# A row-product loop on one core: four larger pieces, two buffers, an even engine split, and semaphores reset in four stages

**Chip, cores, metric.** One core of one Trainium2 chip. The metric is device time in microseconds (us) of one execution; medians of several fast runs unless said otherwise. Runs of one kernel agree here within 0.05%, so differences of one or two us can be read.

## The reference

```python
# inputs: r_inputs, float32, (4096, 256)
dot = jnp.einsum('bi,bj->bij', inputs, inputs)
iu, ju = jnp.triu_indices(256)
return dot[:, iu, ju]            # float32, (4096, 32896)
```

Each row of 256 numbers becomes its 32,896 products x_i * x_j with i <= j. The output is 539 MB, the input 4 MB. So this is a kernel that writes.

## The kernel before

A round takes 256 rows (two per partition). Its 32,896 columns are cut into pieces; for each piece VectorE and ScalarE fill a buffer and SyncE stores it. Round 0 stands ahead of the loop, the other fifteen are its iterations.

```python
REPEAT = 2; PIECES = 6; BUFS = 3; BUDGET = 0.95
...
def split(block, budget):   # the first rows of a piece go to ScalarE until
    ...                     # VectorE's time for the rest is within the budget (ns per output element)
...
borders = even_borders(0, width, PIECES)
x_out = [v.rearrange("(p g r) c -> g p r c", p=P, r=REPEAT)
         for v in dram_disjoint_views(out, PIECES)]
...
def round_of_rows(g, first):
    for c, (lo, hi) in enumerate(zip(borders, borders[1:])):
        o = opool.tile([P, REPEAT, hi - lo], F32, tag=f"o{c % BUFS}", name=f"o{c}")
        ...   # ScalarE: one ACTIVATE per matrix row i and per r;  VectorE: one product for one or two rows i
        dest = x_out[c][bass.ds(g, 1), :, :, a:b].rearrange("o p r c -> p (o r) c")
        nc.sync.dma_start(dest, o[:, :, a - lo : b - lo])
...
with tc.For_i(1, groups, 1, ..., iteration_sync="reg_based") as g:
    copies(xt[:, bass.ds(g, 1)]...)      # x of this round to xv (VectorE) and xa (ScalarE)
    round_of_rows(g, first=False)
```

Of the kernel before, what the change touches and what calls it, by code (L numbers as in the profile page):

```python
# [1 line left out]

# [5 lines left out]

F32 = mybir.dt.float32
AF = mybir.ActivationFunctionType  # L10
ALU = mybir.AluOpType

P = 128
UNIT = 64
REPEAT = 2
PIECES = 6
BUFS = 3
BUDGET = 0.95
FIRST = [512, 1536, 3584]


def even_borders(lo: int, hi: int, pieces: int) -> list[int]:
    units = (hi - lo) // UNIT
    return [lo + units * c // pieces * UNIT for c in range(pieces)] + [hi]


def runs(d: int, lo: int, hi: int) -> list:


    found, at = [], 0  # L30
    for i in range(d):
        a, b = max(at, lo), min(at + d - i, hi)
        if a < b:
            found.append((i, i + a - at, a, b - a))
        at += d - i
    return found


def vector_ops(block: list) -> list:




    ops, k = [], 0
    while k < len(block):
        i, j, at, n = block[k]
        m = 2 if k + 2 < len(block) and i == j else 1
        ops.append((block[k], m))
        k += m
    return ops  # L50


def interleave(block: list) -> list:


    half = len(block)
    while half and len(vector_ops(block[:half])) > len(vector_ops(block[half:])):
        half -= 1
    a, b = vector_ops(block[:half]), vector_ops(block[half:])
    return [op for k in range(max(len(a), len(b))) for ops in (a, b) for op in ops[k : k + 1]]  # L60


def vector_time(block: list) -> float:
    return sum(68 + 1.046 * REPEAT * n * m for (*_, n), m in vector_ops(block))


def split(block: list, budget: float) -> int:


    scalar, k = 0.0, 0  # L70
    while k < len(block):
        scalar += REPEAT * (184 + 0.837 * block[k][3])
        if vector_time(block[k:]) <= budget or scalar > vector_time(block[k + 1 :]):
            break
        k += 1
    return k


def window(ap: bass.AP, free: list) -> bass.AP:
    return bass.AP(ap.tensor, ap.offset, [list(ap.ap[0]), *free])  # L80


@with_exitstack
def kernel(
    ctx: ExitStack, tc: tile.TileContext, x: bass.AP, out: bass.AP
):







    nc = tc.nc
    n, d = x.shape
    width = out.shape[1]
    assert n % (P * REPEAT) == 0 and width == d * (d + 1) // 2 and width % UNIT == 0
    groups = n // (P * REPEAT)
    borders = even_borders(0, width, PIECES)

    xpool = ctx.enter_context(tc.tile_pool(name="x", bufs=1))
    opool = ctx.enter_context(tc.tile_pool(name="o", bufs=1))


    x_out = [
        v.rearrange("(p g r) c -> g p r c", p=P, r=REPEAT)
        for v in dram_disjoint_views(out, PIECES)
    ]


    each, total = REPEAT * d, n // P * d
    xt = xpool.tile([P, groups, each], F32, name="x")
    x_in = x.rearrange("(p g r) d -> p g (r d)", p=P, r=REPEAT)
    xv = xpool.tile([P, each + 1], F32, name="xv")
    xa = xpool.tile([P, each], F32, name="xa")
    nc.vector.memset(xv[:, each:], 0.0)  # L116
    cuts = [0, 1, groups // 2, groups]
    for a, b in zip(cuts, cuts[1:]):
        nc.sync.dma_start(xt[:, a:b], x_in[:, a:b])

    def copies(x_now):
        nc.vector.tensor_copy(xv[:, :each], x_now)  # L122
        nc.scalar.activation(xa, x_now, AF.Copy)  # L123

    def round_of_rows(g, first: bool):
        for c, (lo, hi) in enumerate(zip(borders, borders[1:])):
            o = opool.tile([P, REPEAT, hi - lo], F32, tag=f"o{c % BUFS}", name=f"o{c}")
            start = first and c == 0
            cuts = [lo, *(FIRST if start else []), hi]
            for a, b in zip(cuts, cuts[1:]):  # L130
                block = runs(d, a, b)
                k = split(block, 0.0 if start else BUDGET * REPEAT * (b - a))
                for i, j, at, length in block[:k]:
                    for r in range(REPEAT):
                        nc.scalar.activation(  # L135
                            o[:, r, at - lo : at - lo + length],
                            xa[:, r * d + j : r * d + j + length],
                            AF.Copy,
                            scale=xa[:, r * d + i : r * d + i + 1],
                        )  # L140
                for (i, j, at, length), m in interleave(block[k:]):
                    at -= lo
                    nc.vector.tensor_tensor(  # L143
                        o[:, :, at : at + m * length],
                        window(xv[:, j:], [[d, REPEAT], [1, m], [1, length]]),
                        window(xv[:, i:], [[d, REPEAT], [1, m], [0, length]]),
                        ALU.mult,
                    )
                dest = x_out[c][bass.ds(g, 1), :, :, a:b].rearrange("o p r c -> p (o r) c")
                nc.sync.dma_start(dest, o[:, :, a - lo : b - lo])  # L150

    copies(xt[:, 0])
    round_of_rows(0, first=True)

    with tc.For_i(  # L155
        1,
        groups,
        1,
        hint_engines=[],
        head_align_engines=[mybir.EngineType.DVE, mybir.EngineType.Activation],  # L160
        iteration_sync="reg_based",
    ) as g:
        copies(xt[:, bass.ds(g, 1)].rearrange("p o d -> p (o d)"))
        round_of_rows(g, first=False)


# [1 line left out]
_INS = ["r_inputs"]  # L168
_OUTS = [((4096, 32896), "float32")]


# [20 lines left out]
```

## Time and profile before

| | before |
|---|---|
| median time | 1279.12 us |
| span of the profiled run | 1277.3 us |
| VectorE / ScalarE busy | 79% / 40% |
| DMA engines busy (share of 16 engines' span) | 99.7% |

The span is what the profile shows of one execution; timed runs stand about 2 us above it. The store is the bound: the 16 DMA engines never rest, and the compute engines wait for buffers. The prediction below shows the lines for this. The DMA queue's own waits say what SyncE, which issues every store, waits for (in total, how many times, longest):

```profile
SPq L150 <- DVE o L143: 1183.4, 99, 14.0
SPq L155 <- DMA out_dram<-o: 27.4, 3, 13.0
```

SyncE (SPq) waits for the computing of a piece and for next to nothing else: 4.5 us in all for ScalarE's copies of x, and the very end of the program (L155 is the loop's line). Waiting there is harmless: two stores are already under way or queued.

### The profile page before, as it was taken

The page shows a single profiled execution, that of the slowest core. Times are in us where ns is not written, and L with a number is a line of the kernel's source. Part 1 is how long each engine was busy: PE and PEld are TensorE (multiplying, and loading weights), DVE is VectorE, ACT ScalarE, POOL GpSimd, SP SyncE. Part 2 cuts the span into 40 slices and gives each one's busy share as a digit, 9 for nine tenths or more (in the row PEclk, how much of TensorE's full clock was granted, in tenths as well). Part 3 has the DMA queues.
Part 4 walks back from the last instruction along what each step waited for, and adds up shares of the span by engine and source line. Part 5 has one row for each costly group of instructions (what it writes and reads, how often), then busy time and mean ns, then how long its engine had stood idle before and what let it go on. Part 6 is the DMA issues. An engine that isn't in the chain of part 4 may idle for free.

```text
span 1277.3 us, 6155 instructions
## 1 busy us (share of the span) xinstructions
DVE 1006.2 (79%) x1877; ACT 504.7 (40%) x1591; POOL 0.2 (0%) x4
## 2 busy tenths in 40 slices
DVE  8978787887878788787878878787887878788780
ACT  5433435335252352623526244352433524344340
POOL 0000000000000000000000000000000000000000
DMA  9999999999999999999999999999999999999997
GB/s 385 433 432 430 433 432 429 429 429 428 428 428 429 429 429 428 427 428 429 429 428 428 429 428 429 428 428 428 429 429 429 428 428 429 429 429 427 428 428 327
DMA packets 27365, 543.21 MB, mean 425 GB/s; under 512 B 1632, under 2 KB 1632, under 8 KB 2528
## 3 DMA queue, kind: packets, MB, share of 16 engines
q1 hardware_dynamic: 27360, 543.17, 99.7%
q14 instruction: 5, 0.04, 0.0%
HBM read 4.19 MB, written 538.97 MB: 425 GB/s over the span
## 4 chain that ended last, share of the span: by engine, by line
DMA 67%; ACT 12%; issue 10%; DVE 9%; ACTq 0%; DVEq 0%; SPq 0%
DMA out_dram<-o 67%; ACT o L135 11%; DVE o L143 9%; ACT xa L123 0%; DMA x<-in_r_inputs_dram 0%; ACTq L123 0%; DVEq L143 0%; SPq L150 0%; ACTq L155 0%; ACTq L135 0%; DVE xv L122 0%
## 5 line engine op out<-in xcount | busy, mean ns | idle before, releaser
L143 DVE TENSOR_TENSOR o<-xv 128x760 f32<-128x760 f32 (+56 forms) x1860 | 999.4, 616 | 228.9 <-DMA out_dram<-o 223.1
L135 ACT ACTIVATE o<-xa 128x253 f32<-128x253 f32 (+48 forms) x1574 | 493.3, 403 | 738.5 <-DMA out_dram<-o 707.9
L122 DVE COPY xv<-x 128x512 f32 (+1 forms) x16 | 6.8, 427 | 11.5 <-DVE o L143 7.7
L123 ACT ACTIVATE xa<-x 128x512 f32 (+1 forms) x16 | 10.1, 630 | 3.2 <-DMA x<-in_r_inputs_dram 1.6
L123 ACT ACT_TABLE_LOAD x1 | 1.3, 1283 | 0.7 <-PEq L179 0.7
L116 DVE MEMSET xv<- 128x1 f32 x1 | 0.1, 59 | 0.8 <-PEq L179 0.8
L179 POOL MEMSET const-uint8-127<- 128x1 uint8 x1 | 0.1, 103 | 0.0
L179 POOL MEMSET const-bfloat16-1.0<- 128x1 bf16 x1 | 0.1, 102 | 0.0
L179 POOL MEMSET const-float32-0.0<- 128x1 f32 x1 | 0.1, 99 | 0.2 <-issue 0.2
L179 POOL MEMSET const-float32-1.0<- 128x1 f32 x1 | 0.1, 99 | 0.0
## 6 DMA issues: line engine op xcount, KB each, us to landing
out_dram<-o SPq DMA_DIRECT2D x64, 5504.0 KB, 28.5
out_dram<-o SPq DMA_DIRECT2D x31, 5440.0 KB, 28.9
x<-in_r_inputs_dram SPq DMA_DIRECT2D x1, 2048.0 KB, 12.2
out_dram<-o SPq DMA_DIRECT2D x1, 2048.0 KB, 12.2
out_dram<-o SPq DMA_DIRECT2D x1, 1856.0 KB, 13.8
x<-in_r_inputs_dram SPq DMA_DIRECT2D x1, 1792.0 KB, 6.7
out_dram<-o SPq DMA_DIRECT2D x1, 1024.0 KB, 10.3
out_dram<-o SPq DMA_DIRECT2D x1, 512.0 KB, 9.8
```

What stands on the lines that cost most here:

```text
L116: nc.vector.memset(xv[:, each:], 0.0)
L122: nc.vector.tensor_copy(xv[:, :each], x_now)
L123: nc.scalar.activation(xa, x_now, AF.Copy)
L135: nc.scalar.activation(o[:, r, at - lo : at - lo + length], xa[:, r * d + j : r * d + j + length], AF.Copy, scale=xa[:, r * d + i : r * d ...
L143: nc.vector.tensor_tensor(o[:, :, at : at + m * length], window(xv[:, j:], [[d, REPEAT], [1, m], [1, length]]), window(xv[:, i:], [[d, REP ...
L179: nc = _bacc.Bacc("TRN2", target_bir_lowering=False, num_devices=1)
```

## The change

The intent: fewer, larger packets for the DMA engines; room for the larger buffers by having two of them in place of three; ScalarE takes more of the work, so that a piece is ready in time with two buffers; and the loop's semaphores (the counters by which engines and DMA queues tell each other that something is done) are set back in four stages, one per piece, in place of register arithmetic on every wait.

```diff
-PIECES = 6
-BUFS = 3
-BUDGET = 0.95
+PIECES = 4
+LAST = 7552
+BUFS = 2
+BUDGET = 0.7
...
-    borders = even_borders(0, width, PIECES)
+    borders = [*even_borders(0, width - LAST, PIECES - 1), width]
...
         for c, (lo, hi) in enumerate(zip(borders, borders[1:])):
+            if c and not first:
+                tc.stage_boundary()
...
-        iteration_sync="reg_based",
+        iteration_sync="staggered",
```

## The prediction

> **What bounds the kernel now.** I read the page first (busy shares, slices, queues), then the waits, then one iteration on the timeline, then the windows at the end, then the trace's own packet and landing records. From the page:
>
> ```profile
> DVE 1006.2 (79%) x1877; ACT 504.7 (40%) x1591; POOL 0.2 (0%) x4
> DMA  9999999999999999999999999999999999999997
> ...
> DMA packets 27365, 543.21 MB, mean 425 GB/s; under 512 B 1632, under 2 KB 1632, under 8 KB 2528
> ...
> q1 hardware_dynamic: 27360, 543.17, 99.7%
> q14 instruction: 5, 0.04, 0.0%
> ```
>
> Neither compute engine is full; the 16 DMA engines are busy 99.7% of the span. The waits say the same from the other side:
>
> ```profile
> ACT o L135 <- DMA out_dram<-o: 707.9, 90, 10.1
> DVE o L143 <- DMA out_dram<-o: 223.1, 88, 3.6
> ```
>
> VectorE and ScalarE wait for buffers that the store has not yet released. One iteration on the timeline (piece 0 and piece 5 of 6):
>
> ```profile
> 1091.97 3.29 ACT L135 ACTIVATE o<-xa 128x256 f32<-128x256 f32 x8 [1.97 <-DMA out_dram<-o]
> 1091.99 10.07 DVE L143 TENSOR_TENSOR o<-xv 128x1008 f32<-128x1008 f32 x11 [1.41 <-DMA out_dram<-o]
> ...
> 1157.57 10.96 DVE L143 TENSOR_TENSOR o<-xv 128x340 f32<-128x340 f32 x44 [2.99 <-DMA out_dram<-o]
> 1157.58 10.61 ACT L135 ACTIVATE o<-xa 128x44 f32<-128x44 f32 x40 [7.65 <-DMA out_dram<-o]
> ```
>
> A piece takes VectorE 10 to 11 us; its store takes 16 packets per DMA engine of 0.822 us = 13.15 us. So a gap of about 3 us follows every piece, and the store never runs dry. The end shows one thing more:
>
> ```profile
> 1265.00:1270.00 5.00, 0.00 (x0) 0.00 (x0) 0.00 (x0) 1.00 0.86 370
> 1270.00:1272.00 2.00, 0.00 (x0) 0.00 (x0) 0.00 (x0) 1.00 0.08 33
> 1272.00:1274.00 2.00, 0.00 (x0) 0.00 (x0) 0.00 (x0) 1.00 0.05 22
> 1274.00:1276.00 2.00, 0.00 (x0) 0.00 (x0) 0.00 (x0) 1.00 0.03 11
> ```
>
> The last columns are DMA share and GB/s. 0.06 is one engine of 16: one DMA engine works on alone to 1275.24, while the other fifteen end between 1269.4 and 1270.4 (packet records). **One laggard** sets the end. The sixteen landings of each store show it falling behind by some 0.33 us once per iteration; its packets take 0.84 to 0.85 us instead of 0.813, seen in the iteration I opened while piece 5, the one with many small instructions (84 in 11 us), is computed, and return to 0.82 us when that ends.
>
> **What the Trainium skill says.** "DMA: Bandwidth & Descriptors", section Bandwidth (Where 436 GB/s comes from): 16 ports give 435.2 GB/s. The trace agrees: steady slices hold 427 to 433. Same page, Why small descriptors are slow: each packet carries a fixed overhead. The trace agrees and gives the size: median packets of 2048, 4096 and 8192 B take 84, 159 and 309 ns, so 75 ns per 2048 B (27.3 B/ns) and 9 ns fixed; at 21,760 and 22,016 B the medians are 813 and 822, which is 27.2 B/ns plus 13 ns. Same page, Specifications: about 0.6 us to the first byte on this path. The trace has 1.03 us from the start of the first load's issue (0.74) to its first packet (1.77); I use 1.03. From a last packet to its landing it has 0.44 us (1275.24 to 1275.67). "Runtime: NRT & Kernel Launch", Instruction fetch mechanics: an engine holds 512 instructions and fetches when a branch leaves them. The trace agrees as far as it goes: VectorE runs 235 instructions per iteration, the five instruction packets inside the span all fall before 130 us, and no back edge stalls. The changed loop is shorter on VectorE (about 100) and about 150 on ScalarE, so I expect no fetch stall. I found no page that prices resets in stages.
>
> **The change, part by part.**
>
> (1) Larger pieces. Borders become three of 8448 columns and one of 7552. A packet is one row of a piece: 33,792 or 30,208 B instead of 22,016 or 21,760. Per DMA engine, there were 256 rows x 6 = 1536 output packets; there will be 1024. 512 fewer at 9 to 13 ns is 4.6 to 6.7 us, all of it on the path, because the store is the path. Worked the long way per DMA engine: loads 9.8 us as now; first piece 16 x (0.084 + 0.159 + 0.309 + 0.728) = 20.5; 47 stores x 16 x 1.2555 = 944.1; 16 stores x 16 x 1.1236 = 287.6; start 1.8. Sum 1263.8 us. The same sum for the kernel before is 1269.9, which is where its fifteen engines end. So **minus 6.1 us**.
>
> (2) Two buffers and the even split. Computing piece c+1 may start only when store c-1 has landed, and store c+1 must be queued before store c ends. Prices: a VectorE product takes 68 ns + 1.046 ns per element (piece 0 before: 8844 elements in 11 instructions give 10.0 us, measured 10.07); a ScalarE row takes 184 ns + 0.837 ns per element (8 of 254 give 3.2, measured 3.29). Applied to the new split, VectorE / ScalarE: piece 0: 11.7 / 10.2; piece 1: 11.7 / 11.5; piece 2: 12.5 / 12.2; piece 3: 13.9 / 13.2 us. Before, piece 5 ran both engines side by side for 10.6 us at these prices, so I charge no contention. Piece 0 adds the copies of x (0.43 on VectorE, 0.63 on ScalarE), so 12.1. Around the computing: landing 0.44, first packet 1.03 after the issue, and some 0.5 to 1 us for the stage boundary (my estimate; semaphore steps on SyncE cost 0.05 to 0.1 us each in the tail, and before, computing began 0.1 us after a landing). Cover: store 3 lasts 16 x 1.124 = 18.0 us, the others 20.1. Worst cases: piece 3: 13.9 + 2.2 = 16.1 against 20.1; piece 0: 12.1 + 2.2 = 14.3, with the back edge (0.54 now) 14.9, against 18.0. **Slack 3 to 4 us, so 0 us added.** At the start the loads hold the queue until 13.6 us and the three small chunks until 22.2; the large fourth chunk (4864 columns) is computed by about 17, so nothing is lost there.
>
> (3) Resets in stages. What is removed is 104 register instructions per iteration on VectorE and the old bookkeeping at the back edge, neither of which the store waits for. What is added is, at each of four boundaries, a wait of every engine that the stage two back is finished, with SyncE waiting for the store of two pieces ago. With two buffers that is the very landing the computing waits for anyway. **About 0 us**, some tenths out of the slack of (2).
>
> (4) The laggard: 5.3 us now. If its delay follows bursts of small instructions, the last stage (98 in 14 us, no register instructions) is a gentler burst than 84 plus its register work in 11 us. I take 3.5 us, between 1 and 6: **minus 1.8**.
>
> Sum: 1263.8 + 3.5 + 0.44 landing + 1.6 closing = 1269.3 us of span. Timed runs stand 1.8 us over the profiled span (1279.12 against 1277.3), so 1271.1; I say **1271 us**, 0.6% less.
>
> **The rivals.** (a) A new wait: the boundary costs far more than I think, or computing in pieces 3 and 0 is slower with both engines full. Above 3 to 4 us of excess per stage the store runs dry: every further us in one stage costs 15 us, so 2 us in each of two stages make 1330. For it: two buffers leave only one store queued, and ScalarE goes from 40% to some 60% busy. Against it: the measured piece 5 with both engines full, and 3 us of slack. (b) The packet term fails: large packets run at the same bytes per ns as now, since the overhead might grow with size (9 ns at 8 KB, 13 at 22 KB); then only the laggard moves, and the time is 1275 to 1279. (c) The laggard grows: its cause is not settled by this trace, and a new layout might hit it more often; twice its lag is 1278 or so. With one store queued the fast engines would then idle for it, but the laggard itself would not, so nothing more is added. (d) Faster by 2%, under 1253.5, would need the ceiling itself: 543.17 MB at 435.2 GB/s is 1248 us, plus 1.8 start and 3.8 for landing, closing and timing gives 1253.7. Hardly possible.
>
> **Range and chances.** Without any laggard I get 1267.6; with (b) and the lag of now, 1279. The range is 1266 to 1278. Slower by 2% (above 1304.7) needs (a) at over 25 us in all: 0.05. Faster by 2%: 0.01. The rest, 0.94, is within 2%.
>
> **What would show it.** Right: DMA share 9 in every slice again and 429 to 431 GB/s; median packet of 33,792 B at 1.25 to 1.26 us; VectorE about 800 us and ScalarE about 760 us busy; every computing stage followed by an idle of 4 to 8 us whose releaser is the store (or a stage semaphore that follows it); issue to landing near 26 us; fifteen DMA engines ending near 1264 and one some us later. Wrong: slices with the DMA share at 8 or less (a), packets of 1.262 us or more (b), a single-engine tail longer than 6 us (c), or a boundary that delays the first product by more than 3 us after a landing.

## The result

The changed kernel takes **1295.74 us** (1295.56 to 1295.83), the kernel before 1279.12: 1.3% slower, where 0.6% faster was predicted, and outside the range. The ratio of the fast runs is 1.013 (interval 1.0112 to 1.0147). Ratios here are the mean time of one kernel's fast runs over that of the other's of the same rounds, so not quite the ratio of the medians.

The page of the changed kernel:

```profile
DVE 813.3 (63%) x1607; ACT 772.7 (60%) x2319; POOL 0.2 (0%) x4
...
DMA  9999999999999999999999999999999999999999
GB/s 386 436 432 434 433 394 435 406 419 433 407 435 406 435 428 396 435 406 435 428 398 433 406 435 427 414 418 406 435 425 416 430 395 434 423 418 429 411 419 406
...
q1 hardware_dynamic: 18656, 543.17, 97.9%
q14 instruction: 5, 0.04, 0.0%
```

Busy times came out as predicted (about 800 and 760 us were forecast). The ten-step digits of the DMA row are all 9, as before, and mislead: 9 means 90% or more. The row of rates shows it: every few slices it falls to 394 to 419 GB/s, and the queue is at 97.9% instead of 99.7%. In the kernel before, the slices between the start and the end held 427 to 433:

```profile
GB/s 385 433 432 430 433 432 429 429 429 428 428 428 429 429 429 428 427 428 429 429 428 428 429 428 429 428 428 428 429 429 429 428 428 429 429 429 427 428 428 327
```

What SyncE waits for has changed:

```profile
SPq L153 <- DVE o L146: 664.0, 53, 21.2
SPq L158 <- DMA out_dram<-o: 309.1, 45, 8.6
SPq L153 <- DMA out_dram<-o: 244.1, 14, 17.5
```

L153 is the line that issues a store. Fourteen times, once per iteration after the first, SyncE waits there not for computing but for **another store** to land, 17.5 us at the longest (counted from SyncE's arrival at the line, so most of it is harmless). L158 is the loop's line, the stage boundaries; those 45 waits were foreseen. One such place on the timeline, first all engines, then SyncE alone (start, duration, engine, line, operation):

```profile
634.68 11.83 DVE L146 TENSOR_TENSOR o<-xv 128x972 f32<-128x972 f32 x13
634.77 10.35 ACT L138 ACTIVATE o<-xa 128x256 f32<-128x256 f32 x26
652.35 11.60 ACT L138 ACTIVATE o<-xa 128x138 f32<-128x138 f32 x32 [7.22 <-issue]
652.40 11.80 DVE L146 TENSOR_TENSOR o<-xv 128x820 f32<-128x820 f32 x15 [5.88 <-issue]
```

```profile
651.73 0.37 SPq L153 DMA_DIRECT2D out_dram<-o  x1
```

Piece 0 of this iteration is ready at 634.68 + 11.83 = 646.51. Its store is issued at 651.73, 5.2 us later. In the packet and landing records: the last packet of the iteration before (its piece 3) ends at 651.10, has landed by 651.61, SyncE issues at 651.73, and the first packet of piece 0's store starts at 652.62. For **1.52 us no DMA engine moves anything**. Counted over the whole trace there are 14 such stretches, 1.51 us each on average, 21.1 us in all. The kernel before has none.

The list of the built program's instructions, which is not kept with the runs, names the wait: the loop's first store waits, besides for VectorE and ScalarE, for the count of the semaphore on which the loop's last store arrives. I had read that list before predicting and taken the entry for the load of x, which used the same semaphore earlier. Other builds, most of them never run, point to the rule (from their lists; no trace shows it): the wait stays when the store goes through other views of the output, or is issued by another engine; it is gone when the last stage stores nothing, or when piece 0 goes to another tensor. Of these only the last was run (e5). So in the staged loop the builder seems to order the first store after **all stores of the last stage of the iteration before to the same tensor**, although the pieces are disjoint. With the old resets, by the list, it only waits for the same piece's store of the iteration before, long landed; e1's trace has no wait on a store at the issuing line.

The experiments ask two things: whether this wait is the cause, and what became of the two terms that were to gain (packets and laggard).

### The profile page after: what moved, and what is told of

It is laid out like the page before. It is cut to its first block, busy times and chain, and to the rows that moved or that the text cites. A ratio compares the mean times of both kernels' runs of the same rounds, so it can differ in the third digit from the quotient of the medians.

```text
span 1293.3 us, 5350 instructions
## 1 busy us (share of the span) xinstructions
DVE 813.3 (63%) x1607; ACT 772.7 (60%) x2319; POOL 0.2 (0%) x4
## 3 DMA queue, kind: packets, MB, share of 16 engines
q1 hardware_dynamic: 18656, 543.17, 97.9%
## 4 chain that ended last, share of the span: by engine, by line
DVE 60%; issue 34%; DMA 4%; DVEq 0%; SPq 0%
DVE o L146 59%; DMA out_dram<-o 4%; DVE xv L123 1%; DVEq L158 0%; DMA x<-in_r_inputs_dram 0%; DVEq L123 0%; DVEq L146 0%; SPq L153 0%
## 5 line engine op out<-in xcount | busy, mean ns | idle before, releaser
L146 DVE TENSOR_TENSOR o<-xv 128x284 f32<-128x284 f32 (+62 forms) x1590 | 806.4, 584 | 359.2 <-issue 334.0
L138 ACT ACTIVATE o<-xa 128x215 f32<-128x215 f32 (+4 forms) x2302 | 761.4, 423 | 390.0 <-issue 359.2
## 6 DMA issues: line engine op xcount, KB each, us to landing
out_dram<-o SPq DMA_DIRECT2D x1, 1024.0 KB, 10.3
```

What stands on the lines that cost most here:

```text
L138: nc.scalar.activation(o[:, r, at - lo : at - lo + length], xa[:, r * d + j : r * d + j + length], AF.Copy, scale=xa[:, r * d + i : r * d ...
L146: nc.vector.tensor_tensor(o[:, :, at : at + m * length], window(xv[:, j:], [[d, REPEAT], [1, m], [1, length]]), window(xv[:, i:], [[d, REP ...
```

## The experiments

All but e10 and e12 were timed in rounds with the kernel before (1279.1 to 1279.2 us in each of them), and all their runs were in the fast state; e10 and e12 are single runs, of unknown state. The expectations of e1 and e3 reckon with 1.95 us of dry time, 15 times; measured were 1.51 us, 14 times. "Dry" is the time in which no output packet is under way on any DMA engine, from the packet records.

**e1: pieces, buffers and split, with the old resets.**

```diff
-            if c and not first:
-                tc.stage_boundary()
-        iteration_sync="staggered",
+        iteration_sync="reg_based",
```

> The changed kernel with the resets of the kernel before (no stages): large pieces, two buffers, even split. Theory A (in the staged loop the first store of an iteration waits for the last store of the one before to land, which leaves the DMA engines dry for 1.95 us, 15 times): that wait is gone, so 1263.8 us for fifteen DMA engines, 0.4 landing, 1.6 closing, 1.8 from span to timed run, and 0 to 5 for a laggard: 1268 to 1273 us. Theory B (two buffers leave too little time, or both compute engines full slow each other): the gap stays, 1290 to 1300 us.

Measured: 1277.91 us, ratio 0.999 (0.9974 to 1.0008); no dry stretch. The DMA queue's waits on stores at the issuing line are gone:

```profile
SPq L153 <- DVE o L146: 1205.0, 67, 21.2
SPq L158 <- DMA out_dram<-o: 23.2, 2, 17.8
```

So 17.8 of the 24.6 us above the prediction belong to the staged resets; two buffers and the even split leave no stretch in which all DMA engines are idle. But the time is 5 us above the range expected, which the laggard will explain.

**e2: an attempt to take the wait away, which failed.**

```diff
-                dest = x_out[c][bass.ds(g, 1), :, :, a:b]...
+                dest = x_out[c][bass.ds(g if c else 1, 1), :, :, a:b]...
```

> The changed kernel, staged as it is, but the loop's first store always writes the rows of group 1 (a fixed address, so a wrong result on purpose): the built program then has no wait of that store on the last store of the iteration before; everything else stands. Theory A: 27 us or so go, 1267 to 1273 us. Theory B: 1290 to 1300 us. Theory C (the four stage boundaries themselves cost): only part of the gap goes, 1280 to 1290.

Measured: 1295.14 us, wrong result as intended; 14 dry stretches of 1.47 us. That looked like a defeat of theory A. It was an error of mine: I had filtered the list of waits and missed an entry. The built program still has the wait, and so has the trace: in the iteration shown above SyncE passes it at 651.51 and issues at 651.58.

```profile
SPq L153 <- DMA out_dram<-o: 70.5, 14, 5.1
```

The run says nothing between the theories.

**e3: the staged resets alone**, on the six pieces and three buffers of before, boundaries ahead of pieces 1, 3 and 4.

```diff
+            if c in (1, 3, 4) and not first:
+                tc.stage_boundary()
-        iteration_sync="reg_based",
+        iteration_sync="staggered",
```

> The kernel before (six pieces, three buffers, old split) with resets in four stages. Its built program has the same wait of the first store on the last store of the iteration before. Theory A: plus 15 x 1.95 = 29 us, minus up to 5 us of laggard (all DMA engines meet once per iteration): 1298 to 1308 us. Theory B (the pieces are at fault): within 5 us of 1279.

Measured: 1298.73 us, ratio 1.0155 (1.0138 to 1.0171); 14 dry stretches of 1.48 us, 20.7 us in all. Theory B falls: the pieces are not needed for the loss. The new line among SyncE's waits is there too (28 waits, as the first store waits for both stores of the last stage):

```profile
SPq L152 <- DVE o L145: 840.1, 85, 12.2
SPq L152 <- DMA out_dram<-o: 234.2, 28, 13.0
```

**e4: two such waits per iteration.**

```diff
-                nc.sync.dma_start(dest, o[:, :, a - lo : b - lo])
+                if c == PIECES - 1 and not first:
+                    for r in range(REPEAT):
+                        nc.sync.dma_start(dest[:, r : r + 1], o[:, r : r + 1, a - lo : b - lo])
+                else: ...
```

> The changed kernel with the loop's last store issued as two, one per row of the pair. In the built program the second waits for the first to land, and the next iteration's first store waits for the second: two such waits per iteration in place of one. Theory A: twice the dry time, so plus 15 x 1.95 = 29 us over the changed kernel: 1320 to 1328 us. If a landing wait costs little: within 5 us of 1296.

Measured: 1357.77 us, plus 62 instead of plus 29. There are 29 dry stretches, and they are of two kinds: 1.43 us between the two halves of the last store, as theory A has it, and 4.35 us ahead of the next store. The second kind is new. SyncE works in order: while it waits to issue the second half it cannot pass the next stage boundary, and the compute engines wait for it there:

```profile
653.85 15.10 SPq L155 DMA_DIRECT2D out_dram<-o  x2
669.41 0.63 ACT L124 ACTIVATE xa<-x 128x512 f32 x1 [16.52 <-DMA out_dram<-o]
669.52 0.43 DVE L123 COPY xv<-x 128x512 f32 x1 [15.81 <-issue]
670.08 11.84 DVE L146 TENSOR_TENSOR o<-xv 128x972 f32<-128x972 f32 x13
```

The second half is issued from 668.61 to 668.95 (the line's end, 653.85 + 15.10); only then does piece 0 begin, and its 12 us no longer fit under half a store. Here the two waits cost 5.8 us per iteration, not twice 1.5: a wait on the issuing engine costs more than its own latency when that engine also opens the next stage. The range expected, 1320 to 1328 us, missed this.

**e5: the wait taken away.** In the loop piece 0 is stored to a spare tensor.

```diff
+    aside = nc.dram_tensor("aside", [n, borders[1]], F32, kind="Internal").ap()
-                dest = x_out[c][bass.ds(g, 1), ...
+                dest = (x_out[c] if c or first else aside)[bass.ds(g, 1), ...
```

> The changed kernel, but in the loop piece 0 is stored to a spare HBM tensor of the same row size (wrong result on purpose). This time every wait of the built program was read: the loop's first store no longer waits for the last store of the iteration before; the four stages and their waits stand, bytes and packets are the same. (The earlier trial with a fixed address had kept that wait, which was overlooked.) Theory A (that wait leaves the DMA engines dry): about 1278 us, the time of the pieces with the old resets. Theory C (the stage boundaries themselves cost the time): 1290 to 1296 us.

Measured: 1276.84 us, wrong result on purpose, ratio 0.998 (0.9965 to 0.9998); no dry stretch. The four stages and their boundary waits are still there, and cost nothing:

```profile
SPq L156 <- DVE o L149: 837.1, 67, 21.2
SPq L161 <- DMA out_dram<-o: 248.4, 44, 6.8
SPq L161 <- DMA aside<-o: 113.6, 15, 7.6
```

The stage boundaries (L161) wait for stores 59 times, against 45 in the changed kernel; the issuing line (L156) no longer does. The rate holds as in the kernel before:

```profile
GB/s 384 438 433 431 436 427 440 429 434 428 432 428 427 439 420 435 424 429 424 431 423 435 419 429 424 431 429 428 431 424 429 432 422 424 429 424 431 423 441 348
```

This and e1 settle the cause: theory A holds, theory C falls.

**e6: the wait five times instead of fifteen**, three rounds of rows per iteration.

```diff
-        1, groups, 1,
+        1, groups, 3,
...
-        round_of_rows(g, first=False)
+        for u in range(3): copies(...g + u...); round_of_rows(g + u, ...)   # boundaries after pieces 2, 5, 8 of 12
```

> The changed kernel with three rounds of rows per loop iteration (five iterations instead of fifteen), boundaries after pieces 2, 5 and 8 of 12; the first store of an iteration again waits for the last of the one before. Theory A: 5 dry stretches of 1.4 to 2 us instead of 15, so 14 to 20 us less than the changed kernel, bounded below by the 1278 of the pieces alone: 1278 to 1284 us. If it is the boundaries or the size of the pieces: 1290 to 1296 us, unless only the number of boundaries counts, when it is 1284 too (the spare-tensor run tells those apart).

Measured: 1283.28 us, correct; 4 dry stretches of 1.48 us, 5.9 us in all, as theory A has it: 15.2 us less dry time than the changed kernel, and 12.5 us less time. The slow DMA engine of the next part covers the missing 2.7: the last packet ends at 1279.92, so beyond the 1263.8 us of the sum and the dry time 10.2 us are left for it, against 7.0 in the changed kernel. Instruction packets rise from 5 to 30. The Trainium skill, "Runtime: NRT & Kernel Launch", Instruction fetch mechanics, gives most engines 512 instructions; the trace has 468 per iteration on ScalarE and 333 on VectorE, so this figure alone does not say why, and no run shows that the packets cost time.

**The laggard.** The sum for fifteen DMA engines was 1263.8 us to the last packet. Without any dry time, e1's last packet ends at 1274.06, 10.3 us later, e5's at 1273.19; the kernel before had 5.3 (1275.24 against 1269.9). So the slow engine's delay against the sum nearly doubled, and ate the packets' gain. The tail at the end does not show this; in e1's windows it is as in the kernel before (DMA share and GB/s last):

```profile
1268.00:1270.00 2.00, 0.00 (x0) 0.00 (x0) 0.00 (x0) 1.00 0.60 257
1270.00:1274.00 4.00, 0.00 (x0) 0.00 (x0) 0.00 (x0) 1.00 0.05 23
```

The packet records show why. In e1 the other fifteen engines do not end at 1263.8 either, but at 1269.4 to 1269.6. From 25 to 1262 us the engines stand idle for 6.0 us on average, in the kernel before for 0.3. With two buffers the next piece's computing starts only when the slow engine too has landed (0.1 us after it), so once its lag exceeds the slack the next store comes late for the fast ones: from 639 us on there are moments in every iteration when one engine alone is at work, in the kernel before there are none. So the tail stops growing while the delay does not.

What follows uses the landing records: the time from one store's last landing to the next one's, which is the slow engine's time for that store (means of the iterations from the fourth on). Theory L: bursts of instructions on the compute engines hold that engine up. Theory M: it lags on certain addresses or packets, those of piece 3.

**e7: 24 tiny ScalarE copies per iteration in the kernel before.**

```diff
+                if c == 0 and not first:
+                    for _ in range(DOSE):    # DOSE = 24
+                        nc.scalar.activation(junk_a[:, 8 * _ : 8 * _ + 8], xa[:, :8], AF.Copy)
```

> The kernel before with 24 extra ScalarE copies of 128x8 in piece 0 of each iteration, where ScalarE has 7 us to spare. Theory L (the one slow DMA engine is held up by bursts of ScalarE instructions[...]): 0.1 to 0.2 us per iteration, so 1280.5 to 1282 us, and the store that runs meanwhile takes the slow engine longer by that much. Theory M (the lag belongs to certain addresses or packets): 1279 us.

Measured: 1280.51 us against 1279.18: 1.3 us more (ranges 1280.43 to 1280.63 and 1278.97 to 1279.26; the interval of the ratio, 0.9994 to 1.0027, is wider than these ranges). The dose falls into one place:

```profile
1096.57 2.46 ACT L154 ACTIVATE junk_a<-xa 128x8 f32<-128x8 f32 x24
```

The store under way then takes the slow engine 13.180 us instead of 13.108; the other five differ by 0.006 or less. That is 0.072 us for 24 instructions, **3 ns each**, and 15 x 0.072 = 1.1 of the 1.3 us. Less than the 0.1 to 0.2 expected, but where theory L puts it; ScalarE had time to spare.

**e8 and e11: ScalarE given less, old resets** (e1 with budget 0.85 and 0.95). **e9: the even split alone** (the kernel before with budget 0.7).

> The pieces-only kernel (old resets) with the budget at 0.85 instead of 0.7: VectorE takes more, ScalarE 121 instructions per iteration instead of 144, the last piece as it was. Computing takes up to 14.4 us per piece and the store of piece 3 covers 18.0, so still no dry time. Theory L: the lag falls only where ScalarE's rate falls (pieces 0 to 2, 0.17 us per iteration of 0.55): 1275 to 1277 us. If the even split itself were needed: above 1285 us.

> The pieces-only kernel (old resets) with the old budget of 0.95: VectorE 15.6 to 16.0 us per piece. Piece 0: 15.6 + 0.4 for the copy + 0.5 back edge + 0.1 after landing + 0.4 landing + 1.0 issue = 18.0 against the 18.0 of the store that covers it, so at the edge: 0 to 8 us lost, 1276 to 1285 us. If far more is lost, my sum for the computing is too small; if the time stays at 1276 to 1277, it has slack still.

> The kernel before with the even split alone (budget 0.7 instead of 0.95; six pieces, three buffers, old resets). If the split is free as predicted: 1279 us. Theory L (the slow DMA engine loses about 3 ns per instruction issued in a burst): 38 more instructions per iteration, at most 38 x 3 ns x 15 = 1.7 us: 1279 to 1281 us.

Measured: e8 1277.08 us (ratio 0.9984, 0.9967 to 1.0001; 0.1 us above its range), e11 1277.58 us (0.9987, 0.9981 to 0.9994, with one dry stretch of 0.1 us, in the round ahead of the loop), e9 1280.80 us (1.0013, 1.0006 to 1.0019). So with these pieces the even split is not needed, though at 0.95 it is near the edge, as computed: the fifteen engines end only 1.0 us before the slow one, in e1 4.5. And more instructions cost a little: e9's trace has 569 more products and activations than that of the kernel before, and takes 1.6 us longer; 569 x 3 ns is 1.7. From e1 to e8 there are 298 fewer and 0.8 us less. e11, with 331 fewer still, ends 0.5 us above e8, but it lost 0.8 us ahead of the loop (the last landing of round 0 is at 94.08 us, in e8 at 93.29). e11 settles one thing more. It differs from the kernel before in pieces and buffers alone, and has 171 products and activations **fewer**; yet its last packet ends 10.0 us after the sum, against 5.3. So the number of instructions is not what doubled the delay; larger pieces or two buffers are, and no run tells these two apart. None of these runs has a wait that could explain e9.

**e10: the loop's pieces in another order** (3, 4, 5, 0, 1, 2), one look. **e12: in the order 0, 1, 5, 3, 4, 2**, one look.

```diff
-        for c, (lo, hi) in enumerate(zip(borders, borders[1:])):
+        order = list(enumerate(zip(borders, borders[1:])))
+        for c, (lo, hi) in order if first else [order[i] for i in (0, 1, 5, 3, 4, 2)]:
```

> The kernel before with the loop's pieces in the order 3, 4, 5, 0, 1, 2, for a look at the slow DMA engine. Theory L: the store on which it loses 0.3 us moves with the burst: it is the one under way while piece 5 is computed, two stores before piece 5's own, so now the first of the iteration is computed-for stores shift by three. Theory M (the lag belongs to piece 3's own addresses or packets): it stays on the store of piece 3.

> The kernel before with the loop's pieces in the order 0, 1, 5, 3, 4, 2. In the rotated run the burst still coincided with the store of piece 3, so it told nothing apart; here it coincides with the store of piece 0. Theory L (bursts of instructions hold up one DMA engine): the slow engine needs some 0.25 to 0.3 us more for the store of piece 0, and the store of piece 3 goes back to 13.0 us. Theory M (piece 3's own addresses or packets): the store of piece 3 stays at 13.3 us. Time about 1279 us either way.

e10's text is muddled in its last words; what it meant is that the slow store is the one beside piece 5's computing. The run (1279.01 us) told nothing anyway: turning the order in a circle keeps the burst of piece 5 beside the store of piece 3, which I saw only afterwards. e12 (1278.99 us) tells them apart, by its trace. The slow engine's time per store, in us:

| store of | before | e12 |
|---|---|---|
| piece 0 | 13.00 | **13.23** |
| piece 3 | **13.32** | 13.05 |

Some 0.25 us move from the store of piece 3 (0.27 less) to that of piece 0 (0.23 more), which now runs beside the burst. Piece 3 is as large and goes to the same addresses as before. Theory M falls for this share of the lag. In e1 the slow store is the third of four, the one beside the burst of the last piece: 20.49 us against 20.17 for the other two of its size. The times of e8 and e9 agree with L; the doubled delay is not explained by it. What it is in an instruction that reaches a DMA engine, and whether the recording of instructions has a part in it, these runs don't show.

## Why the prediction was wrong

**Bound, fifteen engines, packets (1).** Right. Median packets measured 1.255 us (33,792 B) and 1.124 us (30,208 B); 1.2555 and 1.1236 were used. The busy time of the packets fell from 1272.8 to 1265.8 us per DMA engine; 6.1 less was forecast.

**Computing and slack (2).** Right. VectorE takes 11.83, 11.80, 12.60 and 14.09 us for the four pieces (11.7, 11.7, 12.5, 13.9 were forecast), with ScalarE busy beside it; piece 0 is ready 5.2 us before its store may go. Rival (a), that computing or boundary outruns the store, is not what happened.

**Resets in stages (3): the step that failed.** It said of the waits added that SyncE waits "for the store of two pieces ago", that this "is the very landing the computing waits for anyway", and priced it at "About 0 us". For the boundaries this holds: computing begins 0.2 to 0.8 us after the landing, and e5 keeps them and loses nothing. What it left out is one more wait, in front of the loop's first store, for the store of **one** piece ago. No computing hides a wait between two consecutive stores: the queue must run dry. Price: landing 0.50, semaphore to issue 0.13, issue to first packet 0.89, so 1.52 us, 14 times, 21.1 us. It was named in the list of the built program, by a semaphore that I took for another's. That the loss stayed within 2%, as the text gave a chance of 0.94, was luck: the text forecast a gain. Rival (a) named the kind (a new wait), but looked for it in excess over the slack, where this one has no slack to eat.

**The laggard (4): mis-sized.** 3.5 us were put, on the thought that the last stage is "a gentler burst". In the changed kernel the last packet ends at 1291.91; less 1263.8 and 21.1 dry, 7.0 us are left for it (in e1, 10.3). So the sign was wrong. ScalarE issues 145 instructions per iteration instead of 99, and the trace has 458 more products and activations than before; at the 3 ns of e7 these are 1.4 us of the 5.0 that e1's laggard has over the one before. The rest is not explained, and e11 shows that the delay grows without extra instructions too. Rival (c) had this size right for the pieces with the old resets (twice the lag, "1278 or so"; e1 took 1277.91), but its sign, a single-engine tail longer than 6 us, would have missed it: the tail is 4.5 us in e1, and 0.3 us or less in the changed kernel, where the fast engines wait for the slow one in every iteration. The "fifteen DMA engines ending near 1264" did not come true in any of these runs.

The sum of the errors: dry 21.1, laggard 3.5; landing and closing 0.6 less (1.43 against 2.04 from the last packet to the end of the span), timed run above the span 0.6 more (2.4 against 1.8): 24.6 us, from 1271.1 to 1295.7. One smaller sum is off too: a loss of 2% needs (a) at 33.7 us counted from 1271, not 25, which holds from 1279 only. The check named for a wrong prediction, slices with the DMA share at 8 or less, would have missed it: the digits stayed 9.

No version found is better by 2%. The pieces with the old resets and a budget of 0.85 (e8) end at 1277.1 us, 0.2% below the kernel before.

## What to carry to other kernels

When one queue of transfers is the bound, ask of each wait in front of an issue how many transfers stay queued behind it: a wait for the transfer just ahead lets the queue run dry by the whole landing and issue time, however early the data is ready (here 1.52 us each), while a wait for the one before that is free as long as computing has slack (e5). Read such waits in the list of the built program, each semaphore followed to its last writer, and count SyncE's own waits by what releases them; the busy row in tenths hid a loss of 1.6% here. And when resets or dependences are moved into stages, check what the loop's first access of a tensor waits for across the back edge.

## What the Trainium skill lacked or had wrong

- No page on what resets in stages wait for. Here the boundaries cost nothing (e5, 1276.84 us), the loop's first store's wait for the last stage's stores 1.52 us, 14 times.
- "DMA: Bandwidth & Descriptors", section Anatomy of one DMA: some 2.0 us of fixed cost per transfer, measured there on another path. From the last packet of one store to the first of one that waits for it, this trace has 1.52 us: 0.50 + 0.13 + 0.89.
- The same page, Specifications: about 0.6 us to the first byte on this path. From the start of the issue to the first packet: 0.89 us (store) and 1.03 us (load).
- The same page, Why small descriptors are slow: about 3 cycles and 32 B per packet. At 27.2 B/ns the packets here show 8 to 9 ns fixed up to 19,456 B, and 13 ns from 21,760 to 33,792 B.
- No page has it that bursts of compute instructions slow one of the 16 DMA engines on a store issued by SyncE: 24 extra ScalarE copies cost it 0.072 us, 3 ns each; a burst of 84 cost 0.3 us per iteration. By what path, no run shows.
- "Runtime: NRT & Kernel Launch", Instruction fetch mechanics, is not contradicted, but its 512 instructions do not explain what the runs show: 5 instruction packets with the short loop, 30 with the unrolled one (e6), which has 468 instructions per iteration on ScalarE.
